# Splitting the last sequence's exponentials between ScalarE and VectorE, with other banks for its feed-forward and shared row scalings

## The chip, the cores and the metric

One core of one Trainium2 chip runs the whole program. The metric is the device time of one execution in microseconds (us). The kernel before took 2112.74 us in the median of 3 runs (2112.03 to 2116.0).

## What is computed

A post-norm decoder layer over 16 sequences of 512 tokens with 256 channels, all in fp32, in three parts that each end in a layer norm of input plus result:

```python
x = _layernorm(x + _L0_attn_ref(x, ...))        # long convolution by poles, gate, gelu MLP (672 wide)
x = _layernorm(x + _L0_xattn_ref(x, ctx, ...))  # causal self-attention + cross-attention
x = _layernorm(x + _L0_ffn_ref(x, ...))         # low-rank FFN, below
# attention: 16 heads of 16 channels; 64 context rows for the cross part
att = jnp.where(causal, q @ k.T * scale, -inf);  y = softmax(att) @ v
y = y + softmax(qc @ kc.T * scale) @ vc;         return y @ Wp + bp
# FFN: 256 -> 64 -> 1024 -> 64 -> 256
P = x @ U1;  H = gelu(P @ V1 + b1);  return (H @ U2) @ V2 + b2
```

The softmax's maximum is subtracted inside the score matmul (a row of the query holds it), so the exponential needs nothing but the scale, and its sum comes out of the next matmul through a column of ones in `va` and `vc`.

## The kernel before

A front part does the convolution for all sequences. Then a list of small operations is made for 16 sequences (`first_block`, `attention`, `ffn` for each `b`) and ordered by a planner. `plan.op(engines, cost, fn, prio, r=, w=)` notes an operation, the engines that may run it ("ACT DVE" means either, with a cost for each), a planned cost in us, a priority (lower goes first) and the buffers that it reads and writes, or parts of them. `Plan.schedule` walks through planned time; whenever an engine is free it takes the ready operation with the lowest priority number whose buffers are free. What comes out is one fixed order per engine. On the chip each engine goes through its own order and waits with semaphores. So a cost that is planned wrongly shows as a wait, and a changed operation can change the order of all that comes after it in planned time, nothing ahead of it. The stages of neighbouring sequences are interleaved: the FFN of sequence `b` runs beside the attention of later ones, and behind the last sequence there is nothing left to interleave with.

The eight PSUM banks of this part are: `scores`, one buffer of four banks `[128, 4 heads, 512]`; `av`, one bank; `mm`, three banks. In SBUF there are three `ex` buffers (128x2048) for exponentials.

Attention of one sequence, heads in four groups of four, two groups `g` and `g + 1` at a time:

- `maxima` (L1362): score matmuls (L1387) into `scores`, for the first and last two sequences copied to `ex` by ScalarE (L1406), masked by GpSimd (L1413), row maxima on VectorE (L1434 to L1445). `shifted` (L1449) turns the maxima (L1455) and adds them to the queries (L1464).
- `sums` (L1470): five fills of `scores` per pair of groups. A fill is a score matmul of four heads (L1491), one exponential of all 128x2048 by ScalarE from PSUM to SBUF (L1503), one or two causal selects by GpSimd (L1514, one for each diagonal block), then the weighted sum into `av` (`wm`, L1526).
- `cross_scores` (L1543) and `cross_sums`: one more fill (L1552, exponential L1563) and its weighted sum into two `mm` banks (L1578). So a sequence has twelve fills and twelve exponentials.
- `copied` (L1589): copies a finished sum out of PSUM (the helper `copy`, L299 on VectorE or L301 on ScalarE). For the last sequence `quotients` follows: PE turns it (L1315), VectorE divides (L1322, L1323) and adds the cross part (L1606). Other sequences divide through DRAM instead (`divided`, L1660).

Then `transposed` (L348), `to_tokens` (L1056, added to the residual at L1067), `layernorm_ops` (L1019: statistics on VectorE L1025 and L1026, four small GpSimd operations L308, L309, L1033, L1034, and one scaling per 256-channel row block on ScalarE, L1041), and `ffn` (L1689): transposes, `U1` (L1704), four times a pair of hidden blocks `hm` (L1716, each block one `mm` bank), gelu on ScalarE (L1724), `qm` into `av` (L1732), then `V2` (L1745), the addition (L1067), the norm and the store (L1757). For the last sequence the norms are done in two halves.

ScalarE holds one table of functions at a time, and exponentials and gelus are in different ones. Therefore all exponentials of a window come before its gelus (the loop at L1773):

```python
for o in gelus[n]:
    o.deps.update(exps[n - 1])
```

The FFNs of the last two sequences (b = 14 and b = 15) share window 17, so both wait for the last sequence's twelfth exponential.

Of the kernel before, what the change touches and what calls it, by code (L numbers as in the profile page):

```python
# [11 lines left out]
ALU = mybir.AluOpType  # L12
# [4 lines left out]
P = 128  # L17
# [180 lines left out]
def decoder_layer(  # L198
# [86 lines left out]
    def dve(n):  # L285
        return 0.16 + n / 960.0
# [729 lines left out]
    gelus_pe = [[] for _ in range(B + 3)]  # L1016
    exps_pe = [[] for _ in range(B + 3)]

    def layernorm_ops(x, prio, at_once=NT):  # L1019
        for c0 in range(0, NT, at_once):  # L1020
            small, cs = Buf("small"), slice(c0, c0 + at_once)
            for c in range(c0, c0 + at_once):

                def stats(e, c=c, small=small):
                    nc.vector.bn_stats(small.t[:, c, 0:6], x.t[:, c, :])  # L1025
                    nc.vector.bn_aggr(small.t[:, c, 6:8], small.t[:, c, 0:6])  # L1026

                plan.op("DVE", 0.6, stats, prio, r=[(x, c)], w=[(small, c)])
            rsqrt_op(small, 7, 1.0, 1e-5, prio, cs)

            def shift(e, small=small, cs=cs):
                st = small.t[:, cs, :]
                nc.gpsimd.tensor_scalar(st[:, :, 9:10], st[:, :, 6:7], -1.0, None, ALU.mult)  # L1033
                nc.gpsimd.tensor_tensor(st[:, :, 9:10], st[:, :, 9:10], st[:, :, 8:9], ALU.mult)  # L1034

            plan.op("POOL", 0.5, shift, prio, w=[small])
            for c in range(c0, c0 + at_once):

                def norm(e, c=c, small=small):
                    st = small.t  # L1040
                    nc.scalar.activation(  # L1041
                        x.t[:, c, :], x.t[:, c, :], AF.Identity, bias=st[:, c, 9:10], scale=st[:, c, 8:9]
                    )

                plan.op("ACT", act(D, True) + 0.05, norm, prio, r=[small], w=[(x, c)])

    def to_tokens(xT, w, res, prio):

# [158 lines left out]
    def attention(b, x_):  # L1207
# [241 lines left out]
        def shifted(g):  # L1449
# [8 lines left out]
            for gg in range(g, g + 2):  # L1458
                q = qs[gg]
                qas[gg], cqas[gg] = Buf("q"), Buf("q")  # L1460
                for row, dst in ((self_rows[gg % 2], qas[gg]), (cross_rows[gg % 2], cqas[gg])):
# [5 lines left out]
                        ps_, r=[ps, q], w=[dst],  # L1467
                    )

        def sums(g0):  # L1470

            av = {g: Buf("av") for g in (g0, g0 + 1)}
            pb_ = p1 + 10 * g0 + 20
            fills = (
                ((g0, 0),), ((g0, 1), (g0, 3)), ((g0, 2), (g0 + 1, 2)), ((g0 + 1, 0),),
                ((g0 + 1, 1), (g0 + 1, 3)),
            )
            left = {g0: (0, 1, 3, 2), g0 + 1: (0, 2, 1, 3)}  # L1480
            wms = {}
            for uses in fills:
                sc, ex = Buf("scores"), Buf("ex")
                kqs = {g: (keys[g], qas[g]) for g, _ in uses}

                def mm(e, uses=uses, sc=sc):
                    at = 0
                    for g, j in uses:
                        for r in range(HPG):
                            hd = bass.ts(r, SLOT)  # L1490
                            nc.tensor.matmul(  # L1491
                                sc.t[:, r, at : at + T - j * P], keys[g].t[hd, TC + j * P : TC + (j + 1) * P],
                                qas[g].t[hd, j * P :], start=True, stop=True,
                            )
                        at += T - j * P

                exps_pe[b + 1].append(plan.op(
                    "PE", sum(tiled(T - j * P) for _, j in uses), mm, p1 + 13,
                    r=[x for kq in kqs.values() for x in kq], w=[sc], tiling=ROWS4, urgent=True,
                ))  # L1500
                exps[b + 1].append(plan.op(
                    "ACT", act(HPG * T),
                    lambda e, sc=sc, ex=ex: nc.scalar.activation(  # L1503
                        ex.t.rearrange("p (r n) -> p r n", r=HPG), sc.t, AF.Exp, scale=scale
                    ),
                    pb_ - 5, r=[sc], w=[ex],
                ))
                at = 0
                for g, j in uses:
                    n = T - j * P  # L1510

                    plan.op(
                        "POOL", 0.65,
                        lambda e, ex=ex, at=at: nc.gpsimd.affine_select(  # L1514
                            out=ex.t.rearrange("p (r n) -> p r n", r=HPG)[:, :, at : at + P],
                            in_=ex.t.rearrange("p (r n) -> p r n", r=HPG)[:, :, at : at + P],
                            compare_op=ALU.is_ge, fill=0.0, base=0,
                            pattern=[[0, HPG], [1, P]], channel_multiplier=-1,
                        ),
                        pb_ - 5, w=[(ex, j + g * NT)],  # L1520
                    )

                    def wm(e, g=g, j=j, n=n, at=at, ex=ex):
                        for r in range(HPG):
                            h = g * HPG + r
                            nc.tensor.matmul(  # L1526
                                av[g].t[bass.ts(r, SLOT), j * P :], va.t[:, j, h * VS : h * VS + SLOT],
                                ex.t[:, r * T + at : r * T + at + n], start=(j == 0), stop=(j == 2 + (g - g0)),
                            )

                    wms[g, j] = (tiled(n), wm, ex)
                    at += n
                for g in (g0, g0 + 1):

                    while left[g] and (g, left[g][0]) in wms:
                        j = left[g][0]
                        cost, wm, ex_ = wms.pop((g, j))
                        plan.op("PE", cost, wm, pb_ - 6, r=[va, (ex_, j + g * NT)], w=[av[g]], tiling=COLS4)
                        left[g] = left[g][1:]
                        if not left[g]:  # L1540
                            copied(av[g], g, 0, pb_ - 7)

        def cross_scores(g):  # L1543

            sc, pb_ = Buf("scores"), p1 + 10 * g + 20
            ex = exc[g] = Buf("ex")

            def cm(e):
                for r in range(HPG):
                    hd = bass.ts(r, SLOT)  # L1550
                    for n in range(2):
                        nc.tensor.matmul(  # L1552
                            sc.t[bass.ts(n, TC), r, :], kcs.t[hd, b % 2, g + n, :], cqas[g + n].t[hd, :],
                            start=True, stop=True,
                        )

            exps_pe[b + 1].append(plan.op(
                "PE", tiled(T) + 0.05, cm, p1 + 13, r=[kcs, cqas[g], cqas[g + 1]], w=[sc], tiling=(SLOT, P // 2),
                urgent=True,
            ))  # L1560
            exps[b + 1].append(plan.op(
                "ACT", act(HPG * T),
                lambda e: nc.scalar.activation(  # L1563
                    ex.t.rearrange("p (r n) -> p r n", r=HPG), sc.t, AF.Exp, scale=scale
                ),
                pb_ - 5, r=[sc], w=[ex],
            ))

        def cross_sums(g):

# [112 lines left out]
        if b == B - 1:  # L1683
            transposed(trip["ytok"], lambda t: t.rearrange("p c h d -> p c (h d)"), p3, yT)
        to_tokens(yT, wp_s, x_, p3)
        layernorm_ops(x_, p3, NT // 2 if b == B - 1 else NT)
        return begun

    def ffn(b, x_):  # L1689
# [16 lines left out]
            plan.op("PE", pe(T), pt, p3 - k, r=[(x2T, k)], w=[ps])  # L1706
        plan.op("ACT DVE", (act(T), dve(T)), lambda e, ps=ps: copy(e, pT.t, ps.t), p3, r=[ps], w=[pT])

        acc = Buf("av")
        for fp in range(NH // 2):  # L1710
            hp = [Buf("mm"), Buf("mm")]

            def hm(e, fp=fp, hp=hp):
                for s in range(2):
                    half = bass.ts(s, RANK)
                    nc.tensor.matmul(hp[s].t, v1_s[half, bass.ts(fp, P)], pT.t[half, :], start=True, stop=True)  # L1716

            gelus_pe[window].append(plan.op("PE", tiled(T), hm, p3, r=[pT], w=hp, tiling=ROWS2))
            hT = [Buf("row"), Buf("row")]
            for s in range(2):  # L1720
                f = 2 * fp + s
                gelus[window].append(plan.op(
                    "ACT", act(T, True),
                    lambda e, f=f, src=hp[s], dst=hT[s]: nc.scalar.activation(  # L1724
                        dst.t, src.t, AF.Gelu_apprx_tanh, bias=b1_s[:, f : f + 1]
                    ),
                    p3, r=[hp[s]], w=[hT[s]],
                ))

            def qm(e, fp=fp, hT=hT):  # L1730
                for s in range(2):
                    nc.tensor.matmul(  # L1732
                        acc.t[bass.ts(s, RANK), :], u2_s[:, 2 * fp + s, :], hT[s].t,
                        start=(fp == 0), stop=(fp == NH // 2 - 1),
                    )

            plan.op("PE", tiled(T), qm, p3 - 1, r=hT, w=[acc], tiling=COLS2)
# [12 lines left out]
            add_op(ps, x_, x_, cp, p4)  # L1750
        halves = 2 if b == B - 1 else 1
        n = NT // halves
        layernorm_ops(x_, p4, n)
        for c0 in range(0, NT, n):
            plan.op(
                "SP", 0.6,
# [110 lines left out]
```

## Time and profile before

| | |
|---|---|
| Median of 3 runs | 2112.74 us |
| The profiled execution's own time | 2110.95 us |
| Its span in the profile | 2109.2 us |
| PE busy (matmul) | 2013.7 us, 95% |
| VectorE busy | 1317.1 us, 62% |
| ScalarE busy | 1020.7 us, 48% |
| GpSimd busy | 758.2 us, 36% |
| Exponentials of self-attention, all sequences (L1503) | 160, mean 1.876 us |
| Clock granted to PE, mean | 0.987 |

The span runs from the first to the last recorded work; 1.75 us of the execution lie around it. A row of the profile's groups names line, engine, operation, output and inputs, shapes, count, busy time, the mean of one in ns, and the idle time of the engine just before it with what ended it. "PEld" is the load of weights into PE, "issue" is time in which the engine waited for nothing that the profile shows. The last sequence's attention begins to use exponentials at 2021.7 us, so that all lines that the diff changes run in the last 88 us of the span (4%).

### The profile page before, as it was taken

To read this page: it belongs to the slowest core of one execution; us is meant where nothing else is said; L and a number is where in the kernel's file an instruction comes from. 1 tells how busy PE (TensorE), PEld (TensorE's weight loads), DVE (VectorE), ACT (ScalarE), POOL (GpSimd) and SP (SyncE) were. 2 spreads that over 40 slices of the span, in tenths; PEclk is the share of its full clock that TensorE was granted. 3 is DMA by queue.
4 is the path that set the end of the run, shared out by engine and by line. 5 is a ranking of instruction groups with operands and counts; after the bars stand their busy time and mean duration, and the time that the engine had idled before them with its cause. 6 is when DMAs were issued, how large, how long until landed. Compare 5 with 4: busy or idle time off the path is not lost.

```text
span 2109.2 us, 35600 instructions
## 1 busy us (share of the span) xinstructions
PE 2013.7 (95%) x14324; PEld 1034.7 (49%) x14324; DVE 1317.1 (62%) x1899; ACT 1020.7 (48%) x1414; POOL 758.2 (36%) x1020
## 2 busy tenths in 40 slices
PE   8899878999999999999999999999999999999977
PEld 4455545444554545454545454544545454545433
DVE  7976522736584848484847575766656675746463
ACT  7764521565426262717172626262535354466664
POOL 6785522243424241414141424242323232334342
PEclk9999989999999999999999999999999999999999
DMA  5366861030304040313131313222221313030300
GB/s 190 112 199 210 272 191 50 1 122 17 117 11 140 14 132 22 122 32 120 34 109 45 106 48 93 61 86 68 72 81 61 93 49 95 19 105 22 102 11 21
DMA packets 114935, 182.16 MB, mean 86 GB/s; under 512 B 13393, under 2 KB 62034, under 8 KB 114642
## 3 DMA queue, kind: packets, MB, share of 16 engines
q1 hardware_dynamic: 113234, 177.26, 27.0%
q10 hardware_dynamic: 1536, 2.62, 0.4%
q8 instruction: 113, 1.85, 0.4%
q14 instruction: 52, 0.43, 0.1%
HBM read 111.09 MB, written 68.76 MB: 85 GB/s over the span
## 4 chain that ended last, share of the span: by engine, by line
PE 81%; ACT 7%; POOL 4%; DVE 3%; issue 3%; DMA 2%; SPq 0%; ACTq 0%; POOLq 0%; DVEq 0%
PE mm L1143 14%; PE scores L1387 10%; PE mm L1296 9%; PE mm L1195 8%; PE scores L1491 7%; PE av L1526 7%; PE mm L1716 4%; PE mm L1224 3%; PE av L1732 3%; PE mm L1056 3%; PE fmm L479 2%; ACT ex L1503 2%; PE mm L1118 2%; PE mm L348 2%; PE mm L1578 2%
## 5 line engine op out<-in xcount | busy, mean ns | idle before, releaser
L1503 ACT ACTIVATE ex<-scores 128x2048 f32<-128x2048 f32 x160 | 300.2, 1876 | 165.4 <-PE scores L1491 161.3
L1143 PE MATMUL mm<-xT,w_l 128*128 128x512 f32 x640 | 298.1, 607 | 0.0
L1514 POOL TENSOR_SCALAR_AFFINE_SELECT ex<-ex 128x512 f32<-128x512 f32 x256 | 158.6, 638 | 355.2 <-ACT ex L1503 330.8
L1387 PE MATMUL scores<-keys,q 32*128 32x320 f32 (+4 forms) x2560 | 224.2, 455 | 11.8 <-ACT ex L1406 10.4
L1491 PE MATMUL scores<-q,keys 32*128 32x512 f32 (+3 forms) x2048 | 185.0, 464 | 17.3 <-ACT ex L1503 14.2
L1724 ACT ACTIVATE row<-mm,b_s 128x512 f32<-128x512 f32 x128 | 81.0, 685 | 233.0 <-PE mm L1716 232.9
L1143 PEld LDWEIGHTS mm<-xT,w_l 128*128 128x128 f32 x640 | 114.9, 190 | 143.7 <-issue 130.8
L1387 PEld LDWEIGHTS scores<-keys,q 32*128 32x128 f32 x2560 | 113.0, 184 | 147.2 <-issue 48.0
L1660 POOL TENSOR_TENSOR nd<-nd,nd 128x1024 f32<-128x1024 f32 x30 | 70.8, 2361 | 307.4 <-DMA nd<-di 307.4
L479 PE MATMUL fmm<-fx,inw 128*128 128x512 f32 x384 | 176.5, 602 | 4.1 <-DVE xv L299 1.5
L1526 PE MATMUL av<-ex,va 128*32 128x512 f32 (+3 forms) x2048 | 170.8, 442 | 0.0
L1432 DVE TENSOR_TENSOR scores<-scores,mask_qk 128x1024 f32<-128x1024 f32 x144 | 126.2, 876 | 63.8 <-PE scores L1387 60.6
L308 POOL TENSOR_SCALAR small<-small 128x4 f32<-128x4 f32 (+1 forms) x66 | 13.3, 201 | 423.0 <-DVE small L1026 393.7
L494 DVE SCALAR_TENSOR_TENSOR frow<-fmm,cw,frow 128x511 f32<-128x511 f32 x192 | 140.5, 744 | 37.7 <-ACT frow L486 33.5
L1195 PE MATMUL mm<-w_l,gT 128*128 128x256 f32 x640 | 160.8, 386 | 0.0
L1155 ACT ACTIVATE row<-mm 128x512 f32<-128x512 f32 x80 | 47.8, 598 | 223.9 <-PE mm L1143 223.9
L1491 PEld LDWEIGHTS scores<-q,keys 32*128 32x128 f32 x2048 | 90.0, 185 | 117.4 <-ACT ex L1503 42.2
L299 DVE COPY row<-av 128x512 f32<-128x512 f32 x68 | 47.1, 692 | 157.9 <-PE av L1526 136.2
L1195 PEld LDWEIGHTS mm<-w_l,gT 128*128 128x128 f32 x640 | 117.8, 190 | 47.3 <-issue 33.7
L1041 ACT ACTIVATE xt<-xt,small 128x256 f32<-128x256 f32 x192 | 103.1, 595 | 76.6 <-POOL small L1034 76.6
L1302 DVE TENSOR_SCALAR q<-mm,bqc_s 128x512 f32<-128x512 f32 x62 | 46.5, 751 | 140.6 <-PE mm L1296 140.6
L1296 PE MATMUL mm<-xT,wqc_s 128*128 128x512 f32 x256 | 129.3, 617 | 0.0
(194 smaller groups left out, 3475.4 us busy)
## 6 DMA issues: line engine op xcount, KB each, us to landing
dn<-row SPq DMA_DIRECT2D x120, 256.0 KB
keys<-dk SPq DMA_DIRECT2D x64, 256.0 KB
nd<-dn SPq DMA_DIRECT2D x30, 512.0 KB
nd<-di SPq DMA_DIRECT2D x30, 512.0 KB
fx<-hpad SPq DMA_DIRECT2D x28, 512.0 KB
xt<-in_x SPq DMA_DIRECT2D x16, 512.0 KB
gate<-gates SPq DMA_DIRECT2D x16, 512.0 KB
yt<-yconv SPq DMA_DIRECT2D x32, 256.0 KB
```

The lines of the kernel that those rows point to most:

```text
L479: nc.tensor.matmul(ps.t, inw[:, k, bass.ts(m, P)], xT.t[:, k, :], start=(k == 0), stop=(k == KD - 1))
L494: lambda e, lag=lag: nc.vector.scalar_tensor_tensor(t.t[:, lag:], ps.t[:, 0 : T - lag], cw[:, m, 2 - lag : 3 - lag], t.t[:, lag:], ALU.mul ...
L1041: nc.scalar.activation(x.t[:, c, :], x.t[:, c, :], AF.Identity, bias=st[:, c, 9:10], scale=st[:, c, 8:9])
L1143: nc.tensor.matmul(ps.t, w[:, k, bass.ts(f, P)], zT.t[:, k, :], start=(k == 0), stop=(k == KD - 1))
L1195: nc.tensor.matmul(ps.t[:, bass.ts(cc, D)], gT.t[:, f, bass.ts(c, P)] if f < NF else gE.t, w_l3[:, f, :] if f < NF else w_l3e[:, c, :], st ...
L1296: nc.tensor.matmul(ps.t, w[:, k, cols], xT.t[:, k, :], start=(k == 0), stop=(k == KD - 1))
L1387: nc.tensor.matmul(sc.t[:, r, at : at + hi - lo], q.t[hd, bass.ts(i, P)], kk.t[hd, lo:hi], start=True, stop=True,)
L1432: nc.vector.tensor_tensor(diag, diag, mask, ALU.add)
L1491: nc.tensor.matmul(sc.t[:, r, at : at + T - j * P], keys[g].t[hd, TC + j * P : TC + (j + 1) * P], qas[g].t[hd, j * P :], start=True, stop= ...
L1503: lambda e, sc=sc, ex=ex: nc.scalar.activation(ex.t.rearrange("p (r n) -> p r n", r=HPG), sc.t, AF.Exp, scale=scale),
L1514: lambda e, ex=ex, at=at: nc.gpsimd.affine_select(out=ex.t.rearrange("p (r n) -> p r n", r=HPG)[:, :, at : at + P], in_=ex.t.rearrange("p ...
L1526: nc.tensor.matmul(av[g].t[bass.ts(r, SLOT), j * P :], va.t[:, j, h * VS : h * VS + SLOT], ex.t[:, r * T + at : r * T + at + n], start=(j ...
```

## The change

For the last sequence alone (b = 15), each of the twelve score fills is no longer read by one exponential. ScalarE takes the first two heads (two of the four banks) as before, straight from PSUM; VectorE copies the other two heads from PSUM to SBUF, into the half of `ex` where they belong; a second exponential on ScalarE then works on this half in place, in SBUF. The next fill needs the first exponential and the copy to be done. The select and the weighted sum need the second exponential.

In the last sequence's FFN the first two pairs of hidden blocks go to the four banks of `scores`, the other two pairs to `mm` as before. The row scaling of the last sequence's two later norms may be run by ScalarE or VectorE; that of b = 14's final norm goes to VectorE (window 17 is greater than 16).

```diff
-    def layernorm_ops(x, prio, at_once=NT):
+    def layernorm_ops(x, prio, at_once=NT, on="ACT"):
...
                 def norm(e, c=c, small=small):
                     st = small.t
+                    if e == "DVE":
+                        nc.vector.tensor_scalar(
+                            x.t[:, c, :], x.t[:, c, :], st[:, c, 8:9], st[:, c, 9:10], ALU.mult, ALU.add
+                        )
+                        return
...
-                plan.op("ACT", act(D, True) + 0.05, norm, prio, r=[small], w=[(x, c)])
+                cost = {"ACT": act(D, True) + 0.05, "DVE": dve(D)}
+                plan.op(on, tuple(cost[e] for e in on.split()), norm, prio, r=[small], w=[(x, c)])
...
+        def exponentials(sc, ex, prio):
+            direct, half = (HPG, None) if b < B - 1 else (HPG // 2, HPG // 2)
+
+            def exp(e, src, rs):
+                dst = ex.t.rearrange("p (r n) -> p r n", r=HPG)
+                nc.scalar.activation(dst[:, rs, :], (sc.t if src else dst)[:, rs, :], AF.Exp, scale=scale)
+
+            if half:
+                rest = slice(direct, HPG)
+                plan.op(
+                    "DVE", dve(half * T),
+                    lambda e: nc.vector.tensor_copy(
+                        ex.t.rearrange("p (r n) -> p r n", r=HPG)[:, rest, :], sc.t[:, rest, :]
+                    ),
+                    prio, r=[(sc, 1)], w=[(ex, "half")],
+                )
+            exps[b + 1].append(plan.op(
+                "ACT", act(direct * T), lambda e: exp(e, True, slice(0, direct)), prio, r=[(sc, 0)] if half else [sc],
+                w=[(ex, "first")] if half else [ex],
+            ))
+            if half:
+                exps[b + 1].append(plan.op("ACT", act(half * T), lambda e: exp(e, False, rest), prio, w=[ex]))
...
-                exps[b + 1].append(plan.op(
-                    "ACT", act(HPG * T),
-                    lambda e, sc=sc, ex=ex: nc.scalar.activation(
-                        ex.t.rearrange("p (r n) -> p r n", r=HPG), sc.t, AF.Exp, scale=scale
-                    ),
-                    pb_ - 5, r=[sc], w=[ex],
-                ))
+                exponentials(sc, ex, pb_ - 5)
...
-        layernorm_ops(x_, p3, NT // 2 if b == B - 1 else NT)
+        layernorm_ops(x_, p3, *((NT // 2, "ACT DVE") if b == B - 1 else ()))
...
-        acc = Buf("av")
+        acc, sc4 = Buf("av"), Buf("scores")
         for fp in range(NH // 2):
-            hp = [Buf("mm"), Buf("mm")]
-
-            def hm(e, fp=fp, hp=hp):
+            in_scores = last and fp < 2
+            hp = [(sc4, 2 * fp + s) for s in range(2)] if in_scores else [Buf("mm"), Buf("mm")]
...
-        layernorm_ops(x_, p4, n)
+        layernorm_ops(x_, p4, n, "ACT DVE" if last else "DVE" if window > B else "ACT")
```

## The prediction

> **What bounds it now.** I began with the stages of the end, because only the last 88 us hold a changed line. In the busy time by stretch the columns are stretch, length, then busy us and count of PE, PEld, DVE, ACT and POOL, the granted clock, DMA share and GB/s:
>
> ```profile
> 2020.00:2025.00 5.00, 1.68 (x12) 0.10 (x8) 4.70 (x9) 3.16 (x2) 0.22 (x2) 0.50 0.00 0
> 2021.70:2063.30 41.60, 32.65 (x337) 14.09 (x338) 18.02 (x41) 27.50 (x21) 15.74 (x25) 0.91 0.04 14
> 2063.30:2087.50 24.20, 20.57 (x101) 10.41 (x100) 11.87 (x31) 11.13 (x18) 5.25 (x11) 1.00 0.00 0
> 2087.50:2097.20 9.70, 9.64 (x32) 2.55 (x32) 0.00 (x0) 6.90 (x12) 1.41 (x3) 1.00 0.16 56
> 2097.20:2109.20 12.00, 1.99 (x8) 1.44 (x8) 4.08 (x11) 2.18 (x4) 2.64 (x8) 0.78 0.12 44
> ```
>
> Second row: the stage of the twelve exponentials. No engine is full: PE 32.65 of 41.6 us, ScalarE 27.5, VectorE 18.0. So it is bound by a chain that goes round. Third: the end of this attention beside b = 14's FFN. Fourth: the last FFN, with PE full by the records and VectorE idle. Fifth: the last norm, a chain of short operations.
>
> The order of time shows the round trip (start, length, engine, line):
>
> ```profile
> 2054.97 1.88 ACT L1503 ACTIVATE ex<-scores 128x2048 f32<-128x2048 f32 x1 [1.32 <-POOL ex L1514]
> ...
> 2056.90 1.15 PE L1491 MATMUL scores<-q,keys 32*128 32x384 f32 x16
> ...
> 2058.20 1.88 ACT L1503 ACTIVATE ex<-scores 128x2048 f32<-128x2048 f32 x1 [1.35 <-PE scores L1491]
> ```
>
> An exponential takes 1.88 us, the fill starts 0.05 later, takes 1.15, and the next exponential starts 3.23 after the last one. There is one `scores` buffer, so neither can run ahead. How often PE really stands still for it, from the list of waits of 2018 to 2066 us (total, times, longest):
>
> ```profile
> PEld scores L1491 <- ACT ex L1503: 8.8, 6, 4.9
> PE scores L1491 <- ACT ex L1503: 5.9, 4, 3.3
> PE scores L1552 <- ACT ex L1503: 0.7, 1, 0.7
> ```
>
> The matmul rows count here: PE loses 6.5 us in five of the eleven refills: 3.32 at 2024.9, 1.00 at 2032.5, 0.50 at 2050.5, 1.06 at 2053.7, 0.65 at 2060.1. At the other six PE has other work until the buffer is free. The starts of the exponentials confirm that: eleven intervals, 38.4 us in sum, from 3.20 up to 4.32, and the long ones are those where PE does turns, transposes and b = 14's L1704 in between.
>
> The chain that ended last shows the two other places:
>
> ```profile
> 2087.54 3.02 PE mm L1716 x8
> ...
> 2094.70 2.50 PE av L1732 x8
> ...
> 2104.92 0.60 ACT xt L1041
> 2105.52 0.49 ACTq L1863
> ```
>
> **What the Trainium skill says.** "ScalarE: Activation LUTs", section "What ACT_TABLE_LOAD costs": an activation with immediate scale and bias costs 186 ns and 0.833 ns per element. For 2048 that is 1.89 us; the trace has 1.88. For 1024 I get an estimate of 1.04; taking half of the columns off the trace's own row gives 1.02. "VectorE: DVE Perf Modes", section "Why PSUM operands drop a tier": a PSUM operand in fp32 runs at one element per cycle. The trace agrees: a copy of 512 from PSUM (L299) takes 692 ns, and a row of 1024 read from PSUM (L1437) 1217 ns. The copy of 1024 is priced at 1.22. "Advanced Engine Details and Errata", section "Bank Collisions": ScalarE and VectorE read PSUM at once at full speed if they use different banks, as the two halves here do. Of one buffer no run here shows it yet; on two `mm` banks L301 (0.59) and L299 (0.69) ran together at 2066.6 at their usual lengths. "TensorE: Matmul & The Clock Gate", Part 1: an idle PE falls to half clock and returns after some 3.4 us of work. The first row above has 0.50, and the first two fills took 2.09 us for 1.15. The idle time ahead of it is in the maxima, which do not change, so I give this no gain.
>
> **The exponentials, step by step.** Removed: 12 activations of 1.88 (22.5 us). Added: 24 of about 1.03 (24.7) on ScalarE and 12 copies of 1.22 (14.6) on VectorE. ScalarE goes to 29.7 us and VectorE to 32.6 of a stage of about 39; neither is full. The buffer comes free when the slower of 1.02 (ScalarE) and 1.22 (VectorE) is done, 0.66 earlier than 1.88. A wait of PE can shrink by no more than itself: 0.66 + 0.66 + 0.50 + 0.66 + 0.65 = 3.1 us. The second exponential ends at 1.22 + 0.05 + 1.04, about 2.3 after the start, against 1.88; so select and weighted sum of each fill come 0.45 later. In the middle the three `ex` buffers take that up in part: behind a fill PE now meets a weighted sum whose select (0.64, two of them 1.24) is not done. Going round once: the sum of fill n ends 4.2 after its first exponential began (2.3 + 0.04 + 1.24 + half a sum 0.55), the fill behind it takes 1.15, and two rounds are 5.4, so 2.7 per round instead of 3.2. That is 0.5 for each of the four free-running refills, which agrees with the 0.5 to 0.66 above. At the twelfth the 0.45 is paid in full, since gelus and cross sum wait for it. Net **-2.6**. Bounds: all of PE's 6.5 goes, less 0.45: -6.0; nothing goes as PE finds no work in time: +0.5.
>
> What queues behind the copy on VectorE is in rival two. Two exponentials instead of one per window add no table load, since both are Exp.
>
> **The FFN in score banks.** No instruction is added. Four pairs of L1716 at 1.06 and four of L1732 at 1.01 are 8.28; from 2087.54 to 2097.20 it took 9.66. The chain has the rest: 3.02 for two pairs that need 2.12, since the second pair lacked a bank until a gelu was through (0.90), and 2.50 for 2.02, the last sum waiting for the last gelus (0.48). With four score banks and three of `mm`, three pairs go at once and the gelus (8 of 0.64, 5.1 us) finish early. **-1.4**; bounds -0.9 (first wait only) and -1.8 (some overlap of the pairs). The `scores` buffer has no other user left.
>
> **Row scalings.** In the attention's norm, GpSimd was ready at 2078.71 and 2080.48, ScalarE had gelus until 2080.13 and scaled four rows from 2080.02 to 2082.08. VectorE on an SBUF row of 256 took 0.35 (L333, one operand less). With two engines all four end near 2081.1: **-1.0**. What is late next is PE, which stands in L1732 until 2081.25 and then does L1745 ahead of the transposes; so 0 to -1.9. At the end the last two rows, 1.09 on ScalarE one after the other, run side by side: **-0.5** (0.4 to 0.6). b = 14's four scalings cost nothing on VectorE: it is idle from 2087.5 to 2097.2, and their store has 10 us to spare. They also leave ScalarE to the gelus.
>
> **Sum:** -2.6 - 1.4 - 1.0 - 0.5 = **-5.5 us** on the profiled 2110.95, which gives 2105.5. The median is 1.79 above the profiled execution, so 2112.74 - 5.5 = **2107.2**. A difference of 0.2%, 4.2 us, is about what a measurement can tell from none.
>
> **Rivals.** *One: PE is the bound.* In the stage PE is busy 32.65 of 41.6 us, and six of eleven refills did not wait for ScalarE at all. If what PE finds missing is then the weighted sum, the exponentials give 0 and the tail -2.9: 2109.8. The same end (about 2110 to 2113) comes if two writers of one `ex` tile are held apart, so that copy and exponential run in turn: 2.3 instead of 1.88 at five refills, +2.1 and 0.45, less 2.9. Against this: ScalarE and VectorE wrote halves of one xT tile at once:
>
> ```profile
> 2070.65 0.69 DVE L299 COPY xT<-mm 128x512 f32<-128x512 f32 x1 [0.38 <-PE mm L348]
> 2071.08 0.59 ACT L301 COPY xT<-mm 128x512 f32<-128x512 f32 x1 [0.20 <-PE mm L348]
> ```
>
> *Two: VectorE's queue (slower).* VectorE works in order, and the copy that frees `scores` may stand behind a copy of `av` (L299) that waits: before, those waited up to 4.7 us at no cost. Then the next fill needs second exponential 1.04, select 1.24, sum 1.07, L299 0.69 and hand-overs, 4.2 after the copy, where it needs 1.2: 3.0 more. All four `av` copies placed so make +12 - 5.5: 2119. It takes four to be slower; two or three end within 0.2%. Against: the planner's prices for copy (1.23), exponential (1.03) and select are near the measured ones, so it places L299 where the sum is nearly done.
>
> *Three: more than summed.* All of PE's waits go, the tail gives its upper bounds: -6.0 - 1.8 - 1.9 - 0.6 = -10.3: 2102.4.
>
> **Chances.** Forecast 0.56 (its own range 2104 to 2109.5: 0.46 of it faster by over 0.2%, 0.10 within); rival three 0.18; rival one 0.17, nearly all within; rival two 0.09. So faster 0.64, within 0.2% 0.27, slower 0.09. The range reaches from rival three to the poor end of rival one: 2102.3 to 2112.3.
>
> **What would show it.** Right: first exponentials and copies of 1.0 and 1.2 us side by side, a round of 2.6 to 2.8 us between free-running refills, last exponential ending 2 to 3 us earlier, the last FFN near 8.3 us on PE with its first three pairs in one run. Wrong: PE waiting for selects (L1514) as long as it waited for L1503; copies of `scores` on VectorE that start over 0.5 us after their fill; or an order in which the cross sum and b = 14's FFN take longer than 24.2 us.

## The result, and the profile after

The change makes the kernel **slower, by 0.2%**: 2117.23 us in the median of 21 runs (2114.14 to 2119.98), against 2112.68 us (2109.32 to 2117.72) for the kernel before in 21 runs beside it. The ratio is 1.002, 95% interval 1.0013 to 1.0026. The forecast was 2107.2, with a range to 2112.3. The profiled execution of the changed kernel was the shortest of its 21; its span is 2112.4 us against 2109.2, so the traces show 3.2 us of the difference of 4.6 between the medians.

The changed kernel has other line numbers. The fills are L1521 (self) and L1576 (cross), both exponentials are L1482, the copy L1488, the select L1538, the weighted sum L1550, the cross sum L1596, the gelu L1747. In the FFN L1739 is `hm`, L1755 `qm`, L1722 `U1`, L1768 `V2`. Row scalings are L1046 on ScalarE and L1042 on VectorE.

First the busy time by stretch of the kernel after, cut where the stages begin and end (columns as in the prediction):

```profile
2021.40:2067.70 46.30, 34.12 (x340) 14.27 (x340) 29.25 (x49) 31.43 (x37) 15.45 (x25) 0.92 0.04 13
2067.70:2091.80 24.10, 21.38 (x97) 10.36 (x96) 11.69 (x30) 9.28 (x14) 5.11 (x9) 0.93 0.00 0
2091.80:2101.00 9.20, 9.16 (x33) 2.72 (x32) 3.17 (x9) 4.84 (x8) 1.65 (x4) 1.00 0.17 59
2101.00:2112.40 11.40, 1.99 (x8) 1.44 (x8) 4.91 (x13) 1.20 (x2) 2.62 (x8) 0.77 0.13 46
```

The stage of the exponentials became longer, 46.3 us instead of 41.6, though no engine is full in it. The attention's end (second row) is as long as before, the last FFN and the last norm are each about 0.5 shorter. So the loss is in the first row, and something in the second ate what the scalings were to bring there.

The order of time of the kernel after shows what happens at a fill:

```profile
2030.90 1.02 ACT L1482 ACTIVATE ex<-scores 128x1024 f32<-128x1024 f32 x1 [0.24 <-PE scores L1521]
...
2031.95 1.23 DVE L1488 COPY ex<-scores 128x1024 f32<-128x1024 f32 x1 [0.47 <-ACT ex L1482]
...
2033.21 1.06 ACT L1482 ACTIVATE ex<-ex 128x1024 f32<-128x1024 f32 x1 [1.29 <-DVE ex L1488]
2033.23 1.14 PE L1521 MATMUL scores<-q,keys 32*128 32x512 f32 x8 [0.74 <-DVE ex L1488]
```

The exponential and the copy read two different halves of `scores`, yet the copy starts only 0.03 us after the exponential has ended, and the bracket names the exponential as what VectorE waited for. So the buffer comes free at 2033.2, 2.3 us after the first read began, where one exponential of 1.88 did it before. The order isn't fixed. Where the copy is first, the exponential waits for it:

```profile
2042.11 1.23 DVE L1488 COPY ex<-scores 128x1024 f32<-128x1024 f32 x1 [0.53 <-PE scores L1576]
...
2043.43 1.02 ACT L1482 ACTIVATE ex<-scores 128x1024 f32<-128x1024 f32 x1 [0.46 <-DVE ex L1488]
```

All twelve fills run in one of these two ways, five with the exponential first and seven with the copy first. The list of waits of 2018 to 2070 us has it in sum (total, times, longest):

```profile
ACT ex L1482 <- DVE ex L1488: 12.7, 12, 1.7
...
DVE ex L1488 <- ACT ex L1482: 7.0, 6, 2.0
...
PE scores L1521 <- DVE ex L1488: 5.0, 4, 2.3
...
PE av L1550 <- POOL ex L1538: 3.4, 6, 0.8
...
PE scores L1521 <- ACT ex L1482: 2.7, 3, 1.2
```

The first row mixes five second exponentials, which need the copied data in any case, with seven first ones, which only wait their turn. In the second row one of the six (1.4 us) stands before a copy that came first; its fill had ended only 0.2 us earlier. PE lost 6.5 us to the exponential before; now it loses 5.0 to the copy and 2.7 to the exponential, 7.7 in sum. It also waits 3.4 us, six times, for selects, where the list of before has no such row for matmuls: the second exponential ends 3.2 us or more after the first read began, where the prediction had 2.3, so the selects are late too. Splitting the work put a hand-over into the round trip instead of shortening it.

The second place is the start of b = 14's gelus, behind the last exponential:

```profile
2067.72 1.28 ACT L1747 ACT_TABLE_LOAD   x1
...
2069.01 1.26 ACT L1747 ACTIVATE row<-mm,b_s 128x512 f32<-128x512 f32 x2
2069.75 2.53 PE L1596 MATMUL mm<-ex,vc 64*32 64x512 f32 x16 [1.95 <-ACT row L1747]
```

The cross sum waits for an `mm` bank that a gelu still reads. A wait there was in the kernel before too, but then the sum took 1.09 us, and here 2.53:

```profile
2065.34 1.09 PE L1578 MATMUL mm<-ex,vc 64*32 64x512 f32 x16 [1.45 <-ACT row L1724]
```

The granted clock of that moment, as a stretch of the kernel after, is 0.71, where the kernel before had 1.00 throughout:

```profile
2070.00:2075.00 5.00, 5.00 (x29) 1.67 (x28) 1.40 (x4) 0.86 (x2) 0.00 (x0) 0.71 0.00 0
```

The third place is the last FFN:

```profile
2091.84 1.99 PE L1739 MATMUL scores<-row,v_s 64*128 64x512 f32 x8
...
2093.88 2.42 ACT L1747 ACTIVATE row<-scores,b_s 128x512 f32<-128x512 f32 x4 [2.21 <-PE scores L1739]
```

Three pairs of hidden blocks do run at once, but the first gelu starts after both pairs of the `scores` buffer are written, although its own bank was full 1 us earlier. In the chain that ended last, the scalings now stand as a single piece, and PE has two gaps in its FFN as before, in other places (start, length, what):

```profile
2091.91 1.92 PE scores L1739 x8
2093.83 0.86 PE mm L1739 x4
2094.69 2.74 PE av L1755 x8
...
2098.48 2.50 PE av L1755 x8
...
2108.66 0.60 ACT xt L1046
```

A table of the same marks in both traces adds up to the span's difference:

| stretch | before, us | after, us | difference |
|---|---|---|---|
| start of the span to the first table load | 2021.70 | 2021.44 | -0.3 |
| table load to end of the twelfth exponential | 41.59 | 46.26 | +4.7 |
| to the start of the cross sum | 2.05 | 2.05 | 0 |
| to the start of `to_tokens` (L1062) | 7.70 | 9.45 | +1.75 |
| to the start of `U1` (the norm's scalings) | 11.95 | 9.97 | -2.0 |
| to the first `hm` of the last FFN | 2.55 | 2.67 | +0.1 |
| to the copy of its result (L299) | 9.68 | 9.16 | -0.5 |
| to the end of the last scaling | 8.79 | 8.26 | -0.5 |

### The profile page after: what moved, and what is told of

Read it like the earlier page. It is cut to its first block, busy times and chain, and to the rows that moved or that the text cites. A ratio compares the mean times of both kernels' runs of the same rounds, so it can differ in the third digit from the quotient of the medians.

```text
span 2112.4 us, 35629 instructions
## 1 busy us (share of the span) xinstructions
PE 2014.7 (95%) x14324; PEld 1034.5 (49%) x14324; DVE 1333.0 (63%) x1917; ACT 1019.5 (48%) x1420; POOL 756.2 (36%) x1020
## 4 chain that ended last, share of the span: by engine, by line
PE 82%; ACT 7%; DVE 3%; POOL 3%; DMA 2%; issue 2%; SPq 0%; ACTq 0%; POOLq 0%; DVEq 0%
PE mm L1149 14%; PE scores L1393 10%; PE mm L1302 9%; PE mm L1201 8%; PE scores L1521 7%; PE av L1550 7%; PE fmm L479 3%; PE mm L1739 3%; PE mm L1230 3%; PE av L1755 3%; PE mm L1062 3%; ACT ex L1482 2%; PE mm L1124 2%; PE mm L1596 2%; PE mm L348 2%
## 5 line engine op out<-in xcount | busy, mean ns | idle before, releaser
L1482 ACT ACTIVATE ex<-scores 128x2048 f32<-128x2048 f32 (+1 forms) x192 | 350.0, 1823 | 193.7 <-PE scores L1521 152.6
L1538 POOL TENSOR_SCALAR_AFFINE_SELECT ex<-ex 128x512 f32<-128x512 f32 x256 | 157.9, 635 | 357.3 <-ACT ex L1482 333.0
L1521 PE MATMUL scores<-q,keys 32*128 32x512 f32 (+3 forms) x2048 | 185.0, 464 | 19.1 <-ACT ex L1482 11.0
L1747 ACT ACTIVATE row<-mm,b_s 128x512 f32<-128x512 f32 x124 | 78.4, 685 | 232.9 <-PE mm L1739 232.9
L1550 PE MATMUL av<-ex,va 128*32 128x512 f32 (+3 forms) x2048 | 170.7, 441 | 3.5 <-POOL ex L1538 3.4
L1521 PEld LDWEIGHTS scores<-q,keys 32*128 32x128 f32 x2048 | 90.0, 185 | 121.7 <-ACT ex L1482 45.4
L1201 PEld LDWEIGHTS mm<-w_l,gT 128*128 128x128 f32 x640 | 117.8, 190 | 47.3 <-issue 33.7
L1046 ACT ACTIVATE xt<-xt,small 128x256 f32<-128x256 f32 x183 | 98.4, 594 | 77.4 <-POOL small L1034 77.4
L299 DVE COPY row<-av 128x512 f32<-128x512 f32 x66 | 45.6, 691 | 140.9 <-PE av L1550 127.7
```

The costliest lines, as they stand in the source:

```text
L1046: nc.scalar.activation(x.t[:, c, :], x.t[:, c, :], AF.Identity, bias=st[:, c, 9:10], scale=st[:, c, 8:9])
L1201: nc.tensor.matmul(ps.t[:, bass.ts(cc, D)], gT.t[:, f, bass.ts(c, P)] if f < NF else gE.t, w_l3[:, f, :] if f < NF else w_l3e[:, c, :], st ...
L1482: nc.scalar.activation(dst[:, rs, :], (sc.t if src else dst)[:, rs, :], AF.Exp, scale=scale)
L1521: nc.tensor.matmul(sc.t[:, r, at : at + T - j * P], keys[g].t[hd, TC + j * P : TC + (j + 1) * P], qas[g].t[hd, j * P :], start=True, stop= ...
L1538: lambda e, ex=ex, at=at: nc.gpsimd.affine_select(out=ex.t.rearrange("p (r n) -> p r n", r=HPG)[:, :, at : at + P], in_=ex.t.rearrange("p ...
L1550: nc.tensor.matmul(av[g].t[bass.ts(r, SLOT), j * P :], va.t[:, j, h * VS : h * VS + SLOT], ex.t[:, r * T + at : r * T + at + n], start=(j ...
```

## The experiments

**Theory A** says that the program, not the chip, holds the two engines apart: the semaphores that it contains order any two engines that use one PSUM buffer, even two that only read and in different banks, and a reader waits for the last write to any part of the buffer. **Theory B** is the form in rival one of the prediction: what is held apart is two writers of one `ex` tile. **Theory C** is rival two, VectorE's queue: the copy comes late because of what stands ahead of it. The first four kernels below ran on one chip together (before: median 2112.3), the other four on another (before: median 2112.4). "Stage" is from the first table load (exponentials) to the second (gelus), "end" from there to the end of the span; the kernel before has 41.6 and 45.9, after 46.3 and 44.7.

### A buffer of its own for the copy (e1)

The edits below are shortened; a line in words stands for several of code.

```diff
+                st = Buf("nd")
-                    lambda e: nc.vector.tensor_copy(ex ... [:, rest, :], sc.t[:, rest, :]),
-                    prio, r=[(sc, 1)], w=[(ex, "half")],
+                    lambda e: nc.vector.tensor_copy(st.t, sc.t[:, rest, :]),
+                    prio, r=[(sc, 1)], w=[st],
...
-   second exponential: ex half -> ex half
+   second exponential: st.t -> ex half
```

> The copy on VectorE goes to a separate SBUF buffer instead of into the half of ex; the second exponential reads that buffer and writes ex. Nothing else is changed. Theory A (any two engines that use one PSUM buffer are put in turn, so the first exponential and the copy of the same scores buffer exclude each other): no difference, the copy still starts at the end of the first exponential, or the other way round, buffer free 2.3 us after the first of the two starts, last exponential ends near 2067.5 us, span about 2112. Theory B (two writers of one ex buffer are put in turn): the two now run side by side, the buffer is free after 1.25 us, the last exponential ends near 2058 us and the span is about 2104. Theory C (the copy is late because other work stands ahead of it on VectorE): as now, but with copies that start after other VectorE work, not at the end of an exponential.

One execution took 2115.55 us; the stage is 47.3. The order of time of this kernel, where VectorE no longer writes to `ex`:

```profile
2022.68 1.02 ACT L1482 ACTIVATE ex<-scores 128x1024 f32<-128x1024 f32 x1
2023.74 1.22 DVE L1489 COPY nd<-scores 128x1024 f32<-128x1024 f32 x1 [1.57 <-ACT ex L1482]
...
2025.00 1.06 ACT L1499 ACTIVATE ex<-nd 128x1024 f32<-128x1024 f32 x1 [1.29 <-DVE nd L1489]
```

The copy starts 0.04 after the exponential ended, as in the changed kernel (0.03). Theory B is false: the `ex` tile is not what holds them apart. `scores` is the only thing that both still use.

### The score banks as two buffers (e2)

The four banks, the instructions and the planner's order rules stay; for the last sequence the banks are two PSUM buffers of two banks instead of one of four.

```diff
+    def bank_of(r):                     # at the last sequence's first fill:
+        if not parts:                   # close the pool of the one buffer, open one with two
...
+            parts.extend(tiles(home, "scores", 2, [P, HPG // 2, T]))
+        return parts[r // 2][:, r % 2]
...
-   matmuls, exponential, copy, FFN use sc.t[:, r]
+   matmuls and FFN use bank_of(r); the exponential reads parts[0], the copy parts[1]
```

> For the last sequence the four banks of scores are two buffers of two banks, one for ScalarE's half and one for VectorE's; the FFN's two pairs of hidden blocks have one each. Same instructions in the same order on every engine. Theory A: copy and first exponential run side by side, free-running rounds of 2.6 to 2.9 us instead of 3.6, last exponential ends at 2058 to 2061 us instead of 2067.7, the first gelu of the last FFN starts behind its own pair (0.9 us earlier), span 2103 to 2107, ratio to before 0.997 to 0.999. Theory B: still in turn, span about 2112, ratio 1.002, only the gelu is earlier. Theory C: between these, copies stand up to 1 us behind other VectorE work, ratio about 1.000.

Median 2107.09 us of 10 runs, ratio 0.9973 (0.9963 to 0.9982): from slower than before to faster than before by this edit alone. The stage is 37.6, the end 44.0. Its order of time:

```profile
2022.93 1.02 ACT L1499 ACTIVATE ex<-scores 128x1024 f32<-128x1024 f32 x1 [1.29 <-PE scores L1538]
2022.93 1.23 DVE L1505 COPY ex<-scores 128x1024 f32<-128x1024 f32 x1 [1.29 <-PE scores L1538]
...
2024.19 1.06 ACT L1499 ACTIVATE ex<-ex 128x1024 f32<-128x1024 f32 x1 [0.23 <-DVE ex L1505]
...
2025.61 1.03 ACT L1499 ACTIVATE ex<-scores 128x1024 f32<-128x1024 f32 x1 [0.36 <-PE scores L1538]
2025.98 1.22 DVE L1505 COPY ex<-scores 128x1024 f32<-128x1024 f32 x1
```

In the first of these fills both start in the same moment when PE is done, both at the usual lengths, and both write halves of the same `ex` tile meanwhile. In the second the copy starts 0.37 later, behind other work on VectorE; no copy of the twelve starts more than 0.5 behind its exponential. The next first exponential comes 2.68 us after the last one. Theory A holds for the reads. The FFN in the same kernel shows it for the writes:

```profile
2080.30 1.99 PE L1756 MATMUL scores<-row,v_s 64*128 64x512 f32 x8
...
2081.47 2.42 ACT L1764 ACTIVATE row<-scores,b_s 128x512 f32<-128x512 f32 x4 [1.35 <-PE scores L1756]
```

The first gelu starts 1.17 us after the first matmul, behind its own pair and beside the second, and from the first `hm` to the copy of the result it takes 8.30 us, where the changed kernel takes 9.16.

### The exponentials undone (e3), and the exponentials alone (e4)

```diff
e3: -   direct, half = (HPG, None) if b < B - 1 else (HPG // 2, HPG // 2)
e3: +   direct, half = HPG, None
e4: -   in_scores = last and fp < 2
e4: +   in_scores = False          # and both norms' scalings on ScalarE alone, as before
```

> One exponential per fill as before the change; the FFN's score banks and the shared row scalings stay. All theories blame the exponentials: the parts left give back what the trace after shows of them, 1.8 us at the attention's norm, 0.5 in the FFN and 0.5 at the last norm: last exponential near 2063.3 us, span 2106 to 2107, ratio 0.9985 to 0.9990. If the loss sits in the FFN or in the scalings instead, the ratio is 1.001 or more.

> Only the exponentials are split; FFN and scalings as before. All theories: the loss is larger than that of the whole change by what the other parts give, 2.8 us: last exponential near 2067.7 us, span 2113 to 2116, ratio 1.002 to 1.004. If the exponentials are not the cause, 1.000.

e3: median 2110.28 of 14 runs, ratio 0.9989 (0.9981 to 0.9997), stage 42.6, end 43.0. e4: median 2119.65 of 5 runs, ratio 1.0039 (1.0027 to 1.0051), stage 48.2, end 47.9. So the change is, within the intervals, the sum of a gain of 0.11% by FFN and scalings, about 2.3 us, and a loss of 0.39% by the split exponentials, about 8 us. e4's own span is 2120.9, above the 2113 to 2116 expected: 6.6 us of the loss are in the stage (48.2 against 41.6) and 2.0 in the end: the cross sum at low clock (2.53 us) is in e4 as well, without any of the other parts. That its stage is 1.9 longer than that of the changed kernel, with the same exponentials, comes with a longer stretch at half clock (see "The clock" below).

### Two buffers, exponentials alone (e6), and one buffer, FFN alone (e7)

e6 is e2 with e4's edits; e7 is the changed kernel with the exponentials (e3's line) and the scalings undone.

> Two buffers of two score banks, the split exponentials alone; FFN and row scalings as before the change. If the split itself gains once the two engines are not put in turn: the stage from table load to last exponential is near 36.5 us against 40.3 before; the end behind it loses 0.5 (second exponential) and up to 2 by the clock: ratio 0.998 to 1.000. If only FFN and scalings carried the gain of the two-buffer kernel: 1.000 to 1.002.

> One buffer of four score banks, one exponential per fill, scalings as before; only the last FFN's first two pairs in score banks. The first gelu should still wait for both pairs, as any reader of the buffer waits for what was last written to it: FFN (first L1739 to the copy) 9.1 to 9.3 us instead of 9.7, ratio 0.9995 to 1.0000. If the wait for the second pair is due to ScalarE's scalings instead, the first gelu starts 0.1 us behind its own pair and the FFN takes 8.3.

e6: median 2107.93 of 10 runs, ratio 0.9982 (0.9971 to 0.9993), stage 37.6, end 47.9. Against e4 that is 0.57%, some 12 us, for the same instructions in two buffers; the traces show 10.6 of them, all in the stage, some 2 of which are e4's longer stretch at half clock. e7: median 2110.49 of 13 runs, ratio 0.9992 (0.9984 to 1.0), stage 42.2, end 45.4, and the FFN takes 9.15 us, so 0.5 of its forecast 1.4. The order of time of e7 has the cause:

```profile
2088.52 1.99 PE L1739 MATMUL scores<-row,v_s 64*128 64x512 f32 x8 [0.68 <-ACT row L301]
...
2090.55 2.42 ACT L1747 ACTIVATE row<-scores,b_s 128x512 f32<-128x512 f32 x4 [2.09 <-PE scores L1739]
```

The first gelu again waits for both pairs. So this part suffers from the single buffer by itself, without split exponentials.

### The cross sum out of the gelus' way (e5, e8)

e5 is e2, e8 the kernel before, each with the last sequence's last cross sum in two score banks instead of two `mm` banks, so that it needn't wait for b = 14's gelus. The expectations call the fall of the clock behind that wait a theory of its own.

```diff
-            cavs = [Buf("mm"), Buf("mm")]
+            if b == B - 1 and g == 2:
+                sc5 = Buf("scores")
+                cavs = [Bank(bank_of, 2 * n, (sc5, n)) for n in range(2)]   # e8: banks 0 and 1
+            else:
+                cavs = [Buf("mm"), Buf("mm")]
```

> As the kernel with two buffers of two score banks, and the last cross sum goes to score banks 0 and 2, which are free by then, instead of two mm banks. If the 2 us between the last exponential and the cross sum, and the half clock behind them, come from the wait for mm banks that b = 14's first gelus hold behind the table load: the cross sum starts within 0.1 us of the last exponential's end, the clock stays at 1.0 there, and the end comes 3 to 4 us earlier than with the two buffers alone: span behind the last exponential 40 to 41 us instead of 44.0, ratio 0.9950 to 0.9965. If something else releases that sum, or the order then puts other work ahead, it stays near 0.997.

> The kernel before, with the last cross sum in score banks 0 and 1 instead of two mm banks, nothing else. If the wait for mm banks holds that sum 2.0 us behind the last exponential (2063.3 to 2065.3 before), it starts within 0.1 us and the end comes 1 to 2 us earlier, ratio 0.9990 to 0.9995. If PE has then to wait for the gelus one step later, the ratio is 1.000.

e5: median 2103.53 of 5 runs, ratio 0.996 (0.9947 to 0.9973), the lowest of all. Stage 37.6 as in e2, end 41.8 instead of 44.0, so 2.2 less, where 3 to 4 were expected. Its interval overlaps with that of e2, so the run times alone don't separate the two; the traces do. In e2's order of time the cross sum waits and is slow; in e5's it runs before the table load is through:

```profile
2058.02 2.53 PE L1613 MATMUL mm<-ex,vc 64*32 64x512 f32 x16 [1.04 <-ACT row L1764]
```

```profile
2056.53 1.64 PE L1629 MATMUL scores<-ex,vc 64*32 64x512 f32 x16
2057.07 1.28 ACT L1780 ACT_TABLE_LOAD   x1
```

The 1.64 includes a wait for the second half of `ex`. The stretches of e5 behind it are at full clock:

```profile
2055.00:2060.00 5.00, 4.65 (x43) 1.53 (x40) 2.94 (x5) 4.63 (x6) 0.27 (x1) 1.00 0.01 3
2060.00:2065.00 5.00, 5.00 (x27) 2.48 (x24) 2.82 (x7) 1.86 (x4) 0.00 (x0) 1.00 0.00 0
```

e8: median 2111.33 of 13 runs, ratio 0.9992 (0.9984 to 1.0), within the forecast; but the end is 45.5 instead of 45.9, 0.4 less, where 1 to 2 were expected. In the kernel before the same edit is worth little:

```profile
2062.72 1.09 PE L1594 MATMUL scores<-ex,vc 64*32 64x512 f32 x16
...
2064.24 1.65 PE L1748 MATMUL av<-row,u_s 128*64 128x512 f32 x4 [0.43 <-ACT row L1740]
```

The cross sum starts 0.5 us behind the twelfth exponential instead of 2.0, but PE then waits 0.43 for the gelu that it waited for before. In the kernel before the clock had not fallen there. In e2 it had: from the cross sum to `to_tokens` e2 takes 9.64 us, where the kernel before takes 7.70. The 2.2 us of e5 are about these 1.9.

## Why the prediction was wrong

**The step that failed** is one sentence: "The buffer comes free when the slower of 1.02 (ScalarE) and 1.22 (VectorE) is done". The two don't overlap in one buffer, so it comes free after their sum, about 2.3 us. The term "Net -2.6" measured +4.7: eleven intervals between fills +3.3, and the twelfth fill +1.35, since its copy and both exponentials end 3.23 after it began instead of 1.88. Even the poor bound, +0.5, was too good, because it supposed the same overlap. The prediction noted "Of one buffer no run here shows it yet", and then set beside it a case on two `mm` buffers. That was the very difference that decided. What the Trainium skill states of the chip in "Advanced Engine Details and Errata", section "Bank Collisions", is confirmed by e2, at 1.02 and 1.23 us; that section says nothing of the order that a program sets. Two of the prediction's signs of being wrong came: copies that start over 0.5 us after their fill (in the five fills with the exponential first), and, with 3.4 us, PE waiting for selects.

**Where the mechanism was right.** With two buffers the term is -4.0 in the stage (37.6 against 41.6), better than -2.6: e2's eleven intervals are 33.88 us instead of 38.42, its last fill 2.41 instead of 1.88. The first two intervals hold 1.67 of those 4.5: the first refill, at half clock in both kernels, began 1.07 us after its exponential instead of 1.93, and full clock came back 3.3 us after that refill instead of 3.9. There the prediction had written "I give this no gain". The round of "2.6 to 2.8" was met in the first free-running ones (2.68 and 2.63). PE's wait for exponentials falls from 6.5 to 1.2 us, and 2.0 come up as waits for selects, as the prediction feared for its middle. The whole of e2, 0.27% or 5.7 us, agrees with the sum of -5.5, partly by luck, as terms were off in both directions.

**The FFN**, -1.4, measured -0.5 with one buffer and -1.4 with two (8.30 us; 8.28 was worked out). It fell to the same cause: "three pairs go at once" came true, but the gelus finish early only when the gelu of the first pair needn't wait for the second.

**The row scalings**, -1.0, measured -2.0, at the other bound (-1.9). VectorE's scaling took 0.35 to 0.41 us, about as priced, beside 0.60 on ScalarE. PE, which was feared to be late behind them, was not: in the changed kernel the transposes come ahead of L1768, where before they stood behind the same matmuls (L1745). **The last norm**, -0.5, measured -0.5.

**What no step had** is +1.75 at the cross sum, through the clock. I looked at the clock only where it was low already.

**The rivals.** Rival one had the right event, "copy and exponential run in turn", but put it on the `ex` tile (refuted by e1), and priced it at 0.42 for each of five refills and 0.45 at the twelfth fill. As the rounds got longer, refills that PE had covered became waits too: seven matmul waits for the two, 7.7 us, where there were five of 6.5. It therefore stopped at 2110 to 2113, and the measured 2117.23 lies beyond the range. Rival two's total of 2119 is near the result, by another road: a copy of `scores` behind a waiting L299 is not what the trace shows. The copies wait for ScalarE or for PE's fill; one alone, at 2053.34, starts some 0.4 us late behind an L299. Rival three didn't occur.

**The clock.** The traces also show when it changes. In the last 100 us of all ten, up to the last matmul, every stretch at half clock lasts 3.41 us or a multiple, and within a trace all of them lie on one grid of 3.41 us; a piece of this grid is called a cell here. One cell at half clock begins within 0.2 us of the cross sum in the changed kernel, and stands at that place in e1, e2, e4 and e6 too; the other five have none there. Three to six such cells stand around the start of the stage in each trace. The cell ahead of the cross sum or around it, as stretches (columns as in the prediction; PE busy is the third number): the kernel before, then the changed kernel with the cell that follows, then e2:

```profile
2062.96:2066.37 3.41, 1.96 (x24) 0.62 (x22) 0.73 (x3) 2.87 (x4) 0.00 (x0) 1.00 0.00 0
2066.13:2069.54 3.41, 0.85 (x12) 0.42 (x4) 1.37 (x3) 3.38 (x4) 0.00 (x0) 1.00 0.00 0
2069.54:2072.95 3.41, 3.20 (x18) 0.69 (x20) 0.52 (x1) 1.28 (x3) 0.00 (x0) 0.50 0.00 0
2054.76:2058.17 3.41, 1.55 (x21) 0.81 (x14) 1.49 (x4) 3.23 (x4) 0.00 (x0) 1.00 0.00 0
```

In the ten traces' last 100 us PE works in 267 cells. Each of the 18 full-clock cells with 1.56 us of work or less is followed by half clock, and each with 1.64 or more by full clock; after a half-clock cell the clock stays low up to 2.82 us of work and returns from 2.91 on. So by these traces the work in a cell counts, and not the length of one wait. In the kernel before, one gap of 1.45 us stands at the cross sum, so no cell there could hold less than 1.96. In the changed kernel the gaps are 0.81 and 1.95 with a turn of 0.66 us between them. In e2 they are 0.81 and 1.04, which leaves 1.56 at the least: there the fall depends on where the grid lies. "TensorE: Matmul & The Clock Gate" of the Trainium skill, Part 1, tells of a free-running window of some 3.4 us that judges this, and these traces agree.

The same cells tell why the stage varies among kernels with the same exponentials. In before, e7, e8 and e3 the half clock lasts until 7.1, 8.4, 9.1 and 9.3 us into the stage, and the stage takes 41.6, 42.2, 42.5 and 42.6. In the changed kernel, e1 and e4 it lasts until 7.1, 12.4 and 16.3, and the stage takes 46.3, 47.3 and 48.2. In the three kernels with two buffers it ends at 5.7 to 6.0, so a part of their gain is clock.

**What stays open.** The rule of the cells is read from ten traces, one of each kernel; no run changes the work in one cell and nothing else, and e5 took the wait and the drop away at once. Where the grid lies differs from trace to trace, so a difference of a microsecond or two in the stage should not be trusted from one. The traces of the changed kernel, e2 and e5 are the shortest of their runs, that of e4 the longest; the ratios rest on all runs.

## What to carry to other kernels

Before two engines are set to share the draining of one PSUM buffer, look whether the trace of before ever shows two engines in one buffer at once; if it does so only in different buffers, give each engine its own, since the order between them comes from the program's semaphores and one buffer with disjoint banks may still be one thing to wait for. The same holds for a producer that fills a buffer in parts: the first reader may wait for the last part. And when a change moves work around a short wait of PE, add up PE's work over 3.41 us around it, the length of a cell here: a wait that cost nothing in clock before can cost more than its own length once that sum falls below about 1.6 us.

## What the runs showed of the hardware that I had not expected

ScalarE and VectorE read two pairs of PSUM banks and wrote two halves of one SBUF tile at the same time at 1.02 and 1.23 us, the lengths that they have one after the other. The chip had the whole gain to give; the program withheld it.

PE fell to half clock although no gap ahead of it was longer than 1.04 us (e2). By the count above it was the work in a cell of 3.41 us that decided, 1.55 there, and the next 16 matmuls took 2.53 us instead of 1.09: a loss larger than the wait.
